# Queries of two heads and two sequences by Strassen's identity, their halves swapped by DMA, with a new plan of the steps

## The chip, the cores and the metric

The kernel runs on one core of a Trainium2 chip. A core has five engines that run their own instruction streams side by side: TensorE (matmul; PE in the profile, its weight loads PEld), VectorE (DVE), ScalarE (ACT), GpSimd (POOL) and SyncE (SP, which here only issues DMAs). The metric is the device time of one execution in microseconds (us), as the median of several runs.

## The reference

All of it is float32. `x` is 16 sequences of 256 tokens by 256. One attention block and one feed-forward block follow each other, each with a layer norm before and after and a residual:

```python
q = (x @ Wq.T).reshape(b, n, H, D)          # H = 16 heads, D = 128
kv_head = cumsum(kv_head * exp(log_f_cumsum), axis=1)
kh, vh = kv_head[..., :H], kv_head[..., H:] # one factor for each token and head
k = einsum('bnd,bnh->bnhd', kp, kh); v = einsum('bnd,bnh->bnhd', vp, vh)
q = rope(q); k = rope(k)
p = softmax(where(mask, einsum('bnhd,bmhd->bhnm', q, k) * scale, -inf))
o = einsum('bhnm,bmhd->bnhd', p, v).reshape(b, n, H * D) @ Wout.T
...
x = x + layernorm(attention(layernorm(x)))
x = x + layernorm(ffn(layernorm(x)))        # ternary weights, silu(gate) * up, rms norm
```

`rope(q)` turns each query: with the halves a and b of its 128 elements, (a cos - b sin, b cos + a sin).

## The kernel before, in words

**Tiling.** The 16 sequences are taken two at a time, in 8 pairs (`Pair`, bp 0 to 7); a pair has 16 heads (`Head`), so there are 128 heads in a row, g = 0 to 127. Operands stand transposed: `xnT` holds a pair's normalised tokens as 128 partitions x 2 chunks of E x 512 columns (256 tokens of each of two sequences). `After` is what follows the attention of one sequence: the output projection (`project_heads`, L833), residual, and the feed-forward block.

**One head.** `queries` (L640) multiplies two 128x128 blocks of `wq_sb` with the two chunks of `xnT` into `qps` in PSUM, 512 columns wide (`contract`, L330; a float32 product is two instructions in the trace). `Rope` (L342) turns it on VectorE: two multiplications with the sine table, each on 64 partitions and from the other half's partitions (L354), one in place with the cosine table (L362), and an addition to `qT` (L365). `keys` (L668) makes `kT` on GpSimd from `kh`, which a DMA of SP brings (`fetch`, L633). `scores` (L672) does four products per head into `sps`; VectorE takes the row minimum with the mask (L695) and ScalarE the exponential (L705). `divide` (L718) divides on ScalarE, `turn` (L738) transposes 32x32 blocks on VectorE (L741) and moves them by DMA through DRAM (`moved`, L748; four `pT`, L754). `scale_values` (L780) makes `vph` on GpSimd, and `outputs` (L788) multiplies into `ops`, which ScalarE copies to `oT` (L813). In pair 0 and the last two heads TensorE does the turning (`on_pe`).

**Order.** The order of every engine's stream is that of the program (`manual_schedule`). `slot(g)` (L1441) is the work of one place in the row of heads: it divides, turns and scales the values of head g - 1, scores head g, makes queries of head g + 1 and keys of head g + 2, rotates the queries of g + 1, and does the outputs of g - 2. All other steps are put in between by `put` (L371): a slot, one of six places in it, and a key, by which the table `MOVED` shifts a step by so many places. DMAs of one engine wait in order: behind a DMA of SP that waits for its data stand all later ones of SP. Per pair and sequence, GpSimd also does the subtraction `lo` (L942), the sums of squares (L960, L1013), normalisations (L308) and residuals (L866, L1063); VectorE does moments (L279), `h` (L931) and `finish` (L1048).

**Buffers.** `heads` has 10 buffers of `oT`, `pT` and `kh` have 3, `xt` (tokens, kept until the last residual) 8, and the four PSUM banks of `ps_mm` are shared by `qps`, `sps`, `gps`, `ups` and others in turn.

**Ternary weights.** During pair 0 `Ternary` (L195) quantises 12 blocks of feed-forward weights: casts and combination on GpSimd (L215, L235 to L238), comparisons on VectorE (L226, L229).

Of the kernel before, what the change touches and what calls it, by code (L numbers as in the profile page):

```python
# [12 lines left out]
MOVED = {  # L13
    "A.fac": 1, "A.y0": 2, "E.fin": 1, "E.mom": -6, "E.nor": 2, "E.pc1": 4, "E.pj0": -1,
    "E.pj1": -1, "E.pj2": 2, "E.pj3": -3, "E.split": 7, "E.sq0": 7, "E.sq1": 3, "E.sq3": 3,
    "E.ss": -3, "E.ssd": -3, "E.sto": 6, "E.tp": 3, "E.up0": -1, "E.up1": -1, "L0": -6,
    "O.fold": 6, "O.g2": -1, "O.g3": -1, "O.gd0": 2, "O.hid1": -2, "O.hid2": -1, "O.lm": 6,
    "O.pj0": -3, "O.pj1": 2, "O.pj3": 3, "O.silu": -3, "O.split": 1, "O.sq0": 1, "O.sq1": 4,
    "O.tp": -1, "O.up0": -3, "O.up1": -3, "O.up2": -7, "O.up3": -3, "P.dec": 2, "P.gate": 2,
    "P.keep0": 1, "P.keep1": 2, "P.kp": -4, "P.ksin": -1, "P.sum": -3, "P.tp0": -2, "P.vhd": 6,  # L20
    "Q.gate": 1, "Q.keep0": 1, "Q.keep1": 4, "Q.kr": -2, "Q.ksin": -2, "Q.mom0": -6,
    "Q.mom1": -3, "Q.nor0": -3, "Q.nor1": 5, "Q.raw": 4, "Q.rows": -3, "Q.sig": -1, "Q.sum": 1,
    "Q.tp0": -1, "Q.tp1": 4, "Q.val": -3, "Q.vh": -6, "Q.vhd": -1, "T0.cb": 1, "T0.ld": -1,
    "T0.ma": -7, "T0.su": 1, "T1.cb": 4, "T1.ld": -4, "T1.ma": -6, "T1.na": -4, "T10.ld": -6,
    "T10.wr": 4, "T11.co": 1, "T11.ma": -2, "T11.na": -3, "T11.su": 1, "T2.ma": -1, "T2.wr": 4,
    "T3.wr": 2, "T4.cb": 1, "T4.ld": 1, "T5.co": 1, "T5.ld": -6, "T5.na": -7, "T7.cb": 1,
    "T7.ld": -3, "T7.ma": -6, "T7.na": -3, "T7.su": -4, "T7.wr": 7, "T8.ld": -10, "T8.su": 1,
    "T8.wr": 7, "T9.ld": -10, "T9.ma": -4, "T9.na": -1, "W0.0": 1, "W0.14": 1, "W1.10": 1,
    "W1.6": -1, "W1.9": 1, "W7.2": -1, "Y12.fin": -4, "Y12.fold": 4, "Y12.nor": 2,
    "Y12.pj0": 3, "Y12.pj1": 2, "Y12.split": 1, "Y12.sq0": 5, "Y12.sq1": 2, "Y12.sq2": -1,  # L30
    "Y12.sq3": 1, "Y12.tp": -7, "Y12.up2": -4, "Y13.nor": 4, "Y13.split": 17,
}

F32 = mybir.dt.float32
BF16 = mybir.dt.bfloat16
F32R = mybir.dt.float32r
AF = mybir.ActivationFunctionType
# [27 lines left out]
def sandwich_kernel(  # L65
# [1375 lines left out]
    def slot(g):  # L1441
# [6 lines left out]
        if before:  # L1448
            before.divide()
# [75 lines left out]
```

## Time and profile before

| | |
|---|---|
| median of 3 runs | 1075.77 us (1074.62 to 1077.19) |
| the profiled execution | 1076.04 us, of which the span from first to last instruction is 1073.8 |
| granted clock of TensorE | 0.997 |
| busy time, us | PE 1058.2, PEld 854.0, DVE 844.8, ACT 734.8, POOL 670.7 |
| DMA | 137.34 MB, mean 128 GB/s |
| 128x512 kT on GpSimd (L670) | 128 of 1.284 us |
| rotation of queries (L354, L362, L365) | 0.688 (64 partitions), 0.700, 0.692 us |

An instruction's row gives its line, engine, operation, the tiles written and read, the shapes, the count, the busy time and the mean in ns of one, and behind a second bar the idle time of its engine ahead of it and what ended that. Matmuls are pipelined: the mean of one is longer than its share of time, so the chain of waits is the better price. "A <- B" in a list of waits says that A's engine idled until B was done; the numbers are the sum in us, the count and the longest.

### The profile page before, as it was taken

How to read it: one execution, taken by the hardware profiler on the slowest of the kernel's cores; microseconds unless marked ns; L12 is line 12 of the kernel's file. 1: busy time of each engine (PE TensorE's matmuls, PEld its weight loads, DVE VectorE, ACT ScalarE, POOL GpSimd, SP SyncE). 2: the span in 40 equal slices, each digit the busy share in tenths (PEclk: the TensorE clock that was granted, in tenths of full speed). 3: DMA queues.
4: the chain of work that ended last, by engine and by line, in shares of the span. 5: the costliest groups of instructions: out<-in, count | busy, mean ns of one | idle time of the engine just before them, and what ended most of it. 6: DMA issues, size and time to landing. Idle time of an engine off the chain costs nothing.

```text
span 1073.8 us, 18504 instructions
## 1 busy us (share of the span) xinstructions
PE 1058.2 (99%) x5730; PEld 854.0 (80%) x5730; DVE 844.8 (79%) x2308; ACT 734.8 (68%) x2152; POOL 670.7 (62%) x705
## 2 busy tenths in 40 slices
PE   8999999999999999999999999999999999999997
PEld 6777776788788877888778887788878888788897
DVE  7888999877887779878798778977788777876565
ACT  4878776676776668576585766866677675857664
POOL 6966897348555676458665585665855546737443
PEclk9999999999999999999999999999999999999998
DMA  7312234553443444444343444435444444443200
GB/s 238 110 51 80 60 121 150 158 162 118 152 143 125 158 130 145 143 130 153 128 157 120 150 140 133 152 130 159 132 137 145 128 142 129 156 133 110 70 11 30
DMA packets 108657, 137.34 MB, mean 128 GB/s; under 512 B 12240, under 2 KB 76240, under 8 KB 108560
## 3 DMA queue, kind: packets, MB, share of 16 engines
q1 hardware_dynamic: 105856, 129.15, 38.0%
q0 software_dynamic: 2000, 6.56, 1.8%
q8 instruction: 46, 0.75, 0.3%
q10 hardware_dynamic: 704, 0.46, 0.1%
q14 instruction: 51, 0.42, 0.1%
HBM read 88.41 MB, written 47.71 MB: 127 GB/s over the span
## 4 chain that ended last, share of the span: by engine, by line
PE 86%; DVE 6%; POOL 4%; ACT 3%; issue 1%; DMA 0%; DVEq 0%; POOLq 0%
PE att L842 18%; PE qps L332 18%; PE sps L682 13%; PE ops L798 9%; PE ffn L997 5%; PE ups L896 5%; PE gps L896 5%; PE ops L805 5%; PE vps L332 1%; PE kp L332 1%; ACT prob L705 1%; DVE prob L695 1%; DVE turned_q L354 1%; PE tps L768 1%; PE tp_f L325 1%
## 5 line engine op out<-in xcount | busy, mean ns | idle before, releaser
L695 DVE CUSTOM_DVE_ANT_0 prob<-sps,mask 128x128 f32<-128x128 f32 (+1 forms) x512 | 160.7, 354 | 117.5 <-PE sps L682 114.7
L813 ACT COPY oT<-ops 128x512 f32<-128x512 f32 x128 | 74.9, 585 | 257.0 <-PE ops L805 256.9
L332 PE MATMUL qps<-xnT,wq_sb 128*128 128x512 f32 x512 | 241.7, 594 | 0.8
L842 PE MATMUL att<-wout_sb,oT 128*128 128x256 f32 x1024 | 237.7, 379 | 0.0
L705 ACT ACTIVATE prob<-prob,low 128x128 f32<-128x128 f32 (+1 forms) x512 | 225.7, 444 | 12.7 <-DVE low L695 12.5
L842 PEld LDWEIGHTS att<-wout_sb,oT 128*128 128x128 f32 x1024 | 188.4, 190 | 30.2 <-issue 8.6
L782 POOL TENSOR_TENSOR vph<-vp,vh 128x512 f32<-128x512 f32 x110 | 115.7, 1052 | 144.6 <-PE ops L805 144.4
L682 PE MATMUL sps<-kT,qT 128*128 128x128 f32 (+1 forms) x1024 | 191.5, 330 | 3.4 <-DVE qT L365 2.5
L354 DVE TENSOR_TENSOR turned_q<-qps,sin_sb 64x512 f32<-64x512 f32 (+1 forms) x258 | 176.0, 682 | 15.7 <-PE qps L332 10.3
L670 POOL TENSOR_TENSOR kT<-kh,kr 128x512 f32<-128x512 f32 x128 | 164.3, 1284 | 8.0 <-PE sps L682 7.7
L734 ACT ACTIVATE even<-prob,total 128x128 f32<-128x128 f32 (+1 forms) x440 | 164.0, 448 | 1.1 <-DVE total L716 1.1
L682 PEld LDWEIGHTS sps<-kT,qT 128*128 128x128 f32 x1024 | 145.1, 191 | 17.0 <-issue 4.0
L332 PEld LDWEIGHTS qps<-xnT,wq_sb 128*128 128x128 f32 x512 | 95.3, 190 | 71.3 <-issue 61.2
L798 PE MATMUL ops<-pT,vph 128*128 128x256 f32 x440 | 131.3, 380 | 0.7 <-POOL lo L942 0.7
L942 POOL TENSOR_TENSOR lo<-h,hi 128x512 fp32r<-128x512 f32 x54 | 68.9, 1276 | 93.4 <-ACT hi L940 84.4
L741 DVE STREAM_TRANSPOSE sq<-even 128x768 f32<-128x768 f32 x110 | 107.4, 976 | 11.1 <-ACT even L734 7.3
L705 ACT ACTIVATION_READ_ACCUMULATOR prob<-prob,low 128x1 f32 x512 | 97.2, 190 | 0.0
L362 DVE TENSOR_TENSOR qps<-qps,cos_sb 128x512 f32<-128x512 f32 (+1 forms) x129 | 89.5, 694 | 4.6
L805 PEld LDWEIGHTS ops<-pT,vph 128*128 128x128 f32 x440 | 83.5, 190 | 11.4
L365 DVE TENSOR_TENSOR qT<-qps,turned_q 128x512 f32<-128x512 f32 (+1 forms) x129 | 88.4, 686 | 4.5
L805 PE MATMUL ops<-pT,vph 128*128 128x128 f32 x440 | 84.5, 274 | 0.0
L798 PEld LDWEIGHTS ops<-pT,vph 128*128 128x128 f32 x440 | 73.8, 191 | 9.3 <-issue 3.4
(177 smaller groups left out, 1894.7 us busy)
## 6 DMA issues: line engine op xcount, KB each, us to landing
moved<-sq SPq DMA_DIRECT2D x110, 384.0 KB, 2.3
pT<-moved SPq DMA_DIRECT2D x440, 96.0 KB, 2.2
kh<-rows SPq DMA_DIRECT2D x126, 256.0 KB, 3.3
xt<-in_x_dram SPq DMA_DIRECT2D x14, 256.0 KB, 2.9
out_dram<-y POOLq DMA_DIRECT2D x13, 256.0 KB, 3.3
wout_sb<-in_wout_dram SPq DMA_DIRECT2D x2, 1024.0 KB, 9.6
w_gu<-in_wgu_dram POOLq DMA_DIRECT2D x8, 256.0 KB, 3.5
wq_sb<-in_wq_dram SPq DMA_DIRECT2D x1, 1536.0 KB, 10.3
```

The lines of the kernel that those rows point to most:

```text
L332: nc.tensor.matmul(ps, lhs[:, c, :], rhs[:, c, :], start=(c == 0), stop=(c == EC - 1))
L354: self.engine.tensor_mul(by_sequence(self.turned[a : a + HALF, :]), by_sequence(self.src[b : b + HALF, :]), over_sequences(sin_sb[b : b + ...
L670: nc.gpsimd.tensor_mul(self.kT, self.kh, self.pair.kr)
L682: nc.tensor.matmul(sps[:, cols], self.qT[:, n0 + i * P : n0 + (i + 1) * P], self.kT[:, n0 : n0 + (i + 1) * P], start=True, stop=True,)
L695: nc.vector.tensor_tensor_reduce(out=prob[:, cols], in0=sps[:, cols], in1=mask[:, P - i * P :], scale=-SCALE, scalar=F32_MAX, op0=ALU.add, ...
L705: nc.scalar.activation(prob[:, cols], prob[:, cols], AF.Exp, bias=low[:, i : i + 1], scale=-1.0, accum_out=self.total[:, b * 2 + i : b * 2 ...
L734: nc.scalar.activation(dst, src, AF.Copy, scale=self.total[:, 2 * b + i : 2 * b + i + 1])
L741: nc.vector.transpose(turned.rearrange("p k u q -> p (k u q)"), self.even.rearrange("p k u q -> p (k u q)"),)
L782: nc.gpsimd.tensor_mul(self.vp, self.pair.vp, self.pair.vh[:, :, self.h : self.h + 1].to_broadcast([P, NT, D]),)
L798: nc.tensor.matmul(ops[:, n0 : n0 + N], self.vp[:, b * (N // P), :], early, start=True, stop=False,)
L805: nc.tensor.matmul(ops[:, n0 + P : n0 + N], self.vp[:, b * (N // P) + 1, :], late, start=False, stop=True,)
L842: nc.tensor.matmul(self.acc[:, t, :], oT[:, n0 + t * P : n0 + (t + 1) * P], wout_sb[:, h, :], start=(h == 0 and t == 0), stop=(h == H - 1) ...
```

## The change

For pairs 1 to 7, heads are taken by twos (`Two`). With the two heads' weights as a 2x2 matrix of blocks (w11 and w12 the two chunks of the first head, w21 and w22 of the second) and the tokens as x11, x12 (first chunk, two sequences), x21, x22 (second chunk), the 2x2 product of blocks takes seven products of 256 columns instead of eight. Four differences of tokens for each pair are made on GpSimd (`token_sums`), and three sums of weights once, on VectorE during pair 0 (`weight_sum`; the sum w21 + w22 overwrites w21 in `wq_sb`).

```diff
+        def first_products(self):
+            self.ps = mm_tile([P, BP, N], f"q1_{self.name}")
+            self.product(self.ps[:, 0, :], w11, x11, True)
+            self.product(self.ps[:, 1, :], w12, x21)
+        def first_out(self):
+            self.part = p1.tile([P, N], F32, tag="part", name=f"part1_{self.name}")
+            nc.scalar.copy(self.part, self.ps[:, 0, :])
+        def first_sum(self):
+            nc.vector.tensor_add(
+                self.heads[0].qT[:, :N], self.ps[:, 1, :], self.part
+            )
+        def second_product(self):
+            self.product(self.ps[:, 0, :], s2, self.pair.sums_of_tokens[1])
+        def second_out(self):
+            self.part = p1.tile([P, N], F32, tag="part", name=f"part_{self.name}")
+            nc.scalar.copy(self.part, self.ps[:, 0, :])
+        def third_products(self):
+            self.ps = mm_tile([P, BP, N], f"q2_{self.name}")
+            self.product(self.ps[:, 0, :], s1, t1, True)
+            self.product(self.ps[:, 1, :], s3, t3)
+        def third_out(self):
+            self.parts = p1.tile([P, BP, N], F32, tag="parts", name=f"parts_{self.name}")
+            nc.scalar.copy(self.parts, self.ps)
+        def third_sums(self):
+            dst = self.heads[1].qT[:, N:]
+            nc.gpsimd.tensor_add(dst, self.parts[:, 0, :], self.parts[:, 1, :])
+            nc.gpsimd.tensor_add(dst, dst, self.part)
+        def last_products(self):
+            self.product(self.ps[:, 0, :], s4, x22)
+            self.product(self.ps[:, 1, :], w22, self.pair.sums_of_tokens[3])
+        def last_sums(self):
+            nc.vector.tensor_add(
+                by_sequence(middle[:, N : 3 * N]),
+                self.ps,
+                over_sequences(self.part, BP),
+            )
+        def swap(self):
+            for half in range(2):
+                a, b = half * HALF, (1 - half) * HALF
+                nc.sync.dma_start(
+                    out=turned_ring[a : a + HALF, :, :],
+                    in_=queries_ring[b : b + HALF, i : i + 2, :],
+                )
```

The queries stand in a ring of four in SBUF (`queries_ring`), and the swapped halves of two heads in `turned_ring`. The second products of a bank add onto the first, which a copy on ScalarE has taken out. The rotation works on SBUF alone:

```diff
+        def rotate(self):
+            q, turned = by_sequence(self.qT), by_sequence(self.turned)
+            nc.vector.tensor_mul(turned, turned, over_sequences(sin_sb, BP))
+            nc.vector.tensor_mul(q, q, over_sequences(cos_sb, BP))
+            nc.vector.tensor_sub(self.qT, self.qT, self.turned)
```

The plan has twelve places in a slot instead of six, and the steps of the heads are put into it as the others are, with keys of their own in `MOVED` (cut here, as is the table, whose old entries are mostly doubled or moved):

```diff
+        two = twos.get(g + 2 + g % 2)
...
+        if two:
+            steps = (
+                (two.third_products, two.third_out),
+                (two.first_products, two.first_out),
+            )[g % 2]
+            for step, name in zip(steps, ("Z", "Zs")):
+                put(g, "begun", step, key=movable(name))
...
+        for b in range(BP):
+            put(g, "scores", lambda b=b: head.scores(b))
+        if two and g % 2:
+            put(g, "begun", two.first_sum, key=movable("Zt"))
+            put(g, "probed", two.second_product, key=movable("Zp"))
+            put(g, "probed", two.second_out, key=movable("Zo"))
+        elif two:
+            put(g, "probed", two.last_products, key=movable("Zp"))
...
+        if two and g % 2 == 0:
+            put(g, "probed", two.last_sums, key=movable("Zo"))
+            put(g, "probed", two.third_sums, key=movable("Zt"))
...
+        if after and g + 1 >= H:
+            put(g, "rotated", after.rotate, key=movable("O"))
...
+        if two and g % 2 == 0:
+            put(g, "rotated", two.swap, key=movable("Zw"))
```

So a two's first and second products stand in the odd slot three before its first head, its third and last products, sums and swaps in the even slot two before, ahead of and behind that slot's scores. Its rotations stand one slot before each head.

Smaller parts:

```diff
-    heads = ctx.enter_context(tc.tile_pool(name="heads", bufs=10))
+    heads = ctx.enter_context(tc.tile_pool(name="heads", bufs=7))
...
-        xts[q] = p3.tile([P, N // P, E], F32, tag="xt", name=f"xt_{q}", bufs=8)
+        xts[q] = p3.tile([P, N // P, E], F32, tag="xt", name=f"xt_{q}", bufs=5)
...
+    def load_again(q):
+        xts[q] = p3.tile([P, N // P, E], F32, tag="xt", name=f"xt2_{q}", bufs=5)
+        nc.sync.dma_start(out=xts[q], in_=x[q].rearrange("(t p) e -> p t e", p=P))
...
-            nc.gpsimd.tensor_copy(self.wb, self.w)
+            nc.scalar.copy(self.wb, self.w)
...
-            nc.gpsimd.tensor_sub(up, up, self.dn)
+            nc.vector.tensor_sub(up, up, self.dn)
...
-            turned = p2.tile([P, 4, 3 * BP, 32], F32, tag="sq32", name=f"sq32_{self.tag}")
+            turned = p1.tile([P, 4, 3 * BP, 32], F32, tag="sq32", name=f"sq32_{self.tag}")
...
-            self.pT = p3.tile([P, 4, 3 * BP, 32], F32, tag="pT", name=f"pT_{self.tag}")
+            self.pT = p2.tile([P, 4, 3 * BP, 32], F32, tag="pT", name=f"pT_{self.tag}")
...
-                nc.vector.tensor_scalar(
+                nc.scalar.activation(
                     self.y[:, t, :],
                     self.acc[:, t, :],
-                    rs[:, t : t + 1],
-                    nb[:, t : t + 1],
-                    ALU.mult,
-                    ALU.add,
+                    AF.Identity,
+                    bias=nb[:, t : t + 1],
+                    scale=rs[:, t : t + 1],
                 )
```

Tokens are loaded a second time for the residual (`load_again`, in the slot 17 after a pair's start), which frees their first buffer. The last step is `finish`, which goes from VectorE to ScalarE. The tiles `xhi` and `xlo` have one buffer each instead of two, apart from two of the last sequences, which take the buffers of `xnT`. The ones are a single column that is broadcast, and ten warm-up products of 128 columns replace five of 256.

## The prediction

> **What bounds the kernel now.** I read the share of each engine first, then the busy time by stretch, then the chain of work in one pair's steady part, then the costs by shape.
>
> ```profile
> PE 1058.2 (99%) x5730; PEld 854.0 (80%) x5730; DVE 844.8 (79%) x2308; ACT 734.8 (68%) x2152; POOL 670.7 (62%) x705
> ...
> PE 86%; DVE 6%; POOL 4%; ACT 3%; issue 1%; DMA 0%; DVEq 0%; POOLq 0%
> ```
>
> TensorE is busy 99% and carries 86% of the chain. The busy time by stretch (after each stretch's length: PE, PEld, DVE, ACT, POOL) shows where it is not full:
>
> ```profile
> 120.00:188.00 68.00, 65.47 (x312) 48.76 (x312) 62.50 (x163) 47.33 (x151) 58.40 (x57) 1.00 0.37 117
> ...
> 445.00:573.20 128.20, 128.04 (x696) 103.74 (x695) 102.45 (x282) 87.86 (x257) 80.61 (x85) 1.00 0.44 140
> ```
>
> A pair of 16 slots lasts 128.2 us (8.01 us a slot) and TensorE idles 0.16 us of it. From 120 to 188 us, with VectorE busy 62.5 of 68 us (92%) and GpSimd 58.4 (86%), TensorE idles 2.5 us (3.7%). The waits of that stretch name the cause, and the chain from 502 us on has the prices of matmuls:
>
> ```profile
> PEld sps L682 <- DVE qT L365: 2.7, 3, 2.0
> ```
> ```profile
> 507.70 3.45 PE att L842 x16
> ...
> 512.46 1.31 PE sps L682 x8
> ```
>
> Every f32 product is two instructions. Sixteen of 256 columns take 3.45 us, 0.2156 each; four query instructions of 512 take 1.72 in the chain of waits, 0.430 each. So time goes by columns, and a 256-column instruction is half a 512-column one; its weight load (190 ns) fits beneath it.
>
> **The products.** Two heads take 8 instructions of 512 columns now, 8 x 0.430 = 3.44 us, and 14 of 256 afterwards, 14 x 0.2156 = 3.02. That is 0.42 us for two heads; 56 such twos in pairs 1 to 7 give **-23.6 us**, and a pair would last 128.2 - 8 x 0.42 = 124.8. Six more weight loads for two heads (190 ns) would cost 1.1 us if bare; the att row, with a new weight for each instruction, excludes that. Pair 0 keeps its products.
>
> **VectorE.** The groups by shape in 445 to 573.2 us:
>
> ```profile
> L354 DVE TENSOR_TENSOR turned_q<-qps,sin_sb 64x512 f32<-64x512 f32 x32 | 22.0, 688 | 1.2 <-PE qps L332 0.5
> ...
> L362 DVE TENSOR_TENSOR qps<-qps,cos_sb 128x512 f32<-128x512 f32 x16 | 11.2, 700 | 0.6
> L365 DVE TENSOR_TENSOR qT<-qps,turned_q 128x512 f32<-128x512 f32 x16 | 11.1, 692 | 0.6
> ```
>
> These 44.3 us go, and the 1.9 us of finish (L1053) move to ScalarE. Added per pair: 48 rotations of 128x512 at 0.69 (33.1 us), 8 sums of 256 columns at 0.42 (3.4) and 8 of 512 at 0.69 (5.5). Together 102.4 - 46.2 + 42.0 = 98.2 of 124.8 us. On the face of it VectorE gets lighter.
>
> But the kind of operand changes: the old steps read qps in PSUM and one table in SBUF, the rotations read two tensors in SBUF. The trace has a few such instructions beside a busy GpSimd, the compare steps of the ternary weights (minimum, median, maximum ns):
>
> ```profile
> L226 DVE SCALAR_TENSOR_TENSOR t_gu<-t_gu x8: 691/706/1746, 34.1 to 109.2; 128x512 bf16<-128x512 bf16 x8
> ```
> ```profile
> L229 DVE SCALAR_TENSOR_TENSOR t_p<-t_p x4: 684/1372/2059, 124.0 to 152.9; 128x512 bf16<-128x512 bf16 x4
> ```
>
> The one of 1746 ns began at 102.09 us, 0.1 us after a kT on GpSimd (101.99, 1.29 us), and ended at 103.84, 0.56 after kT's end; those with GpSimd idle take 0.69. They stand in line for each other, and GpSimd stretches too: the kT at 153.93 took 1.72 instead of 1.28. Over the 24 of L226 and L229 the mean is (7.8 + 8.4 + 2.8 + 5.5)/24 = 1.02 us, 0.33 above 0.69. The bounds for a rotation are therefore 0 and 1.3 us of waiting (a whole kT); I take 0.33, since GpSimd was about as busy then (88.0 of the first 120 us, 58.4 of the next 68) as it will be. That is 48 x 0.33 = 15.8 us, so VectorE holds 114 of 124.8 us (91%): its spare time falls from 1.6 to 0.7 us a slot.
>
> The Trainium skill (SBUF — State Buffer, Who interferes with whom) says that a VectorE instruction with two SBUF inputs and a GpSimd instruction that reads SBUF block each other for the whole instruction. By it alone GpSimd's 95.2 us and 33.1 of rotations would follow one another, 128.3 us a pair, and nothing would be gained. The trace agrees for the big operations; the subtraction at 1039.92 us took 0.68 beside a GpSimd pow of 0.71, so small ones do not hold it.
>
> **GpSimd.** Per pair 16 adds and 4 token differences of 128x256 at 0.73 (row of L1013, 724 to 732 ns): 80.6 + 14.6 = 95.2 us (76%). Nothing on the path if kT, vph and the third sums stay within their slot of slack; an even slot carries 1.28 + 1.46 + 1.05 and 2.8 of feed-forward work, 6.6 of 7.8 us.
>
> **ScalarE.** Per two, two copies of 256 columns (0.46, the PSUM row of L773) and one of 512 (0.585, L813): 12 us a pair, with finish (4 x 0.57) 102 of 124.8 us; it idles 35.7 us a pair for ops now, which hides them. One is on a path: the last products add into the bank that third_out reads. Third products take 0.86 us, the scores 1.31, so the copy must end by 2.17 us in the slot. It begins near 1.06 and ends near 1.65; with one feed-forward cast (0.61) ahead, 2.26. I take 0.05 us for each two, 2.8 in all (bounds 0 and 0.5 each, 28).
>
> **SP and the swaps.** SP's list shows, for the slot whose scores start at 504.5 us, the fetch at 505.03, moved at 507.58 and the four pT from 509.96 to 511.70, 7.2 us in. Divide and turn come 1.5 us later after the change (0.86 of products, 0.59 of copy), so SP reaches the swaps at 8.7; issues of 0.38 each, and a landing of 3.3 (the kh row, 256 KB each as well), end at 12.7. The rotation's place in the next slot is 7.8 + 4.5 = 12.3: 0.4 us late, of which nothing waits on TensorE yet: three rotations (2.07 + 1.0) end at 15.8, and the scores that need them start at 15.6 + 0.86 = 16.5. Behind the swaps on SP stand the next fetch and moved (due at 12.1), which are not held up. I take 0; the ends are 0 (it can only add) and 34 (rival 3). The reloads of x (16 of 256 KB, 2.9 us) and fewer buffers of oT, pT, xt and sq32 cost nothing: the loads are asked for three slots ahead, pT is written one slot after its predecessor's reader; uncovered, one reload would cost its 2.9 us.
>
> **Pair 0, start and end.** Eight sums of weights (0.69, 5.5 us) and 12 ternary differences come to VectorE, which idles 20.6 of the first 120 us; hidden, and 5.5 us if not. Casts leave GpSimd (12 x 0.6) for ScalarE, idle 32 us there. The end's steps keep their order; single buffers of xhi and xlo may hold a split for some tenths: 0, at most 1 us.
>
> **What becomes late.** The scores wait for qT where VectorE is crowded. The one wait of 1.8 us (164.2 us, the hand-over between pairs, with statistics of four tiles ahead of the rotation) is what VectorE at 92% cost. I put one such wait into each of the seven pairs, less the 0.86 us of products that now stand ahead of the scores: 7 x 0.95 = 6.7 us. Ends: the steady stretch's 0.16 us a pair (1.1 in all), and 3.7% of 7 x 124.8 (32 us).
>
> **Sum**, against the profiled execution's own 1076.04 us (span 1073.8 and 2.2 around it; 0.27 over the median 1075.77): 1076.0 - 23.6 + 6.7 + 2.8 = 1061.9, less the 0.3 to the median: **1061.6 us**.
>
> **Rivals.**
> 1. *All of it is hidden*: rotations wait for GpSimd only in spare time. 1075.8 - 23.6 + 1.1 = 1053. For it: 0.7 us a slot stays spare, and scores now have products ahead. Against: the waits at 92%.
> 2. *The shared access of VectorE and GpSimd becomes the bound*, slower than before. If a rotation waits half a kT (0.64 us), VectorE needs 98.2 + 30.7 = 128.9 us a pair, 0.7 over now: 1081; by the idle share of 120 to 188 us, 1075.8 - 23.6 + 32 = 1084. I put it at 1083. It decides from 0.62 us of mean wait, where 98.2 + 48 w reaches 128.2. For it: maxima of 2.06 us. Against: half the rows at 0.69.
> 3. *The swaps come late*: if they land in 4.6 us (rows of the first loads) and 0.7 of slack is used up, each two costs 0.6 us, 34 in all: 1086.
> 4. *It gives back what it takes*: waits of some 24 us, 1076.
>
> Chances: forecast 0.40 (own range 1054 to 1071), rival 1 0.24, rival 2 0.24, rival 3 0.06, rival 4 0.06. Faster by over 0.2% (2.2 us, about what a measurement here tells from no change): 0.64; within 0.06; slower 0.30. The range takes rival 1's floor less one us of luck at the ends, 1051, and from rivals 2 and 3 all but the worst, to 1090.
>
> **What would show it.** Right: qps groups of 256 columns, about 784 instructions at 0.216 in the chain, a steady pair of 125 to 127 us, rotations with means near 1.0 us and maxima of 1.7 to 2.1, and TensorE idle before sps with qT as releaser. Wrong: rotations at 0.69 throughout (rival 1), means above 1.3 with VectorE over 95% (rival 2), VectorE waiting for the swap's DMA (rival 3), or last products waiting for the copies. A different clock would void the sum.

## The result and the profile after

The changed kernel takes 1154.38 us (median of 4 runs, 1149.02 to 1156.4) against 1075.19 for the kernel before beside it (4 runs): a ratio of 1.0726, 95% interval 1.0683 to 1.0769. It is slower by 79 us, where 14 us less (1061.6) were forecast. The profiled execution took 1156.24 us, of which the span is 1154.5.

The page of the changed kernel, engine shares and chain of waits:

```profile
PE 1067.5 (92%) x6076; PEld 920.5 (80%) x6076; DVE 913.1 (79%) x2302; ACT 821.5 (71%) x2358; POOL 835.8 (72%) x821
...
PE 39%; DVE 25%; POOL 14%; DMA 9%; ACT 7%; issue 4%; SPq 2%; DVEq 0%; POOLq 0%; ACTq 0%
```

TensorE's part of the chain fell from 86 to 39%. No other engine is full: VectorE is busy 79%, as before. So this is no engine that became the bound, but a chain through several engines that TensorE now waits for. The busy time of one steady pair (pair 4; columns as in the stretches above):

```profile
582.80:718.00 135.20, 127.24 (x744) 111.77 (x744) 108.64 (x278) 99.62 (x285) 107.53 (x104) 1.00 0.56 168
```

It lasts 135.2 us, not 128.2, and TensorE is without work for 8.0 us of it. The rotations and kT, by shape over the whole span:

```profile
L820 POOL TENSOR_TENSOR kT<-kh,kr 128x512 f32<-128x512 f32 x128 | 182.8, 1430 | 0.3
...
L815 DVE TENSOR_TENSOR queries_ring<-queries_ring,cos_sb 128x512 f32<-128x512 f32 x112 | 128.2, 1144 | 0.0
...
L816 DVE TENSOR_TENSOR queries_ring<-queries_ring,turned_ring 128x512 f32<-128x512 f32 x112 | 123.2, 1100 | 3.9
...
L814 DVE TENSOR_TENSOR turned_ring<-turned_ring,sin_sb 128x512 f32<-128x512 f32 x112 | 97.7, 873 | 40.9 <-DMA turned_ring<-queries_ring 40.9
```

A rotation step takes (873 + 1144 + 1100)/3 = 1039 ns, near the 1.02 of the prediction, and kT 1430 instead of 1284. The last row has what the prediction put at nothing: VectorE idles 40.9 us for the swap's DMA. The list of waits says for whom that matters (sum in us, count, longest):

```profile
PE sps L832 <- DVE total L868: 25.4, 23, 2.9
...
PE sps L832 <- DVE queries_ring L816: 14.6, 12, 3.2
PE q L675 <- DVE queries_ring L702: 12.0, 15, 3.1
```

The scores (sps) wait for the last step of a rotation (L816). The first line is the same wait: in all 23 cases L868, a reciprocal of 0.17 us, stands directly behind L816 on VectorE, and the wait is put down to what came last. The timeline of one slot of pair 4 shows the whole chain, for SyncE, VectorE, GpSimd and TensorE (start, duration, line, tiles; idle time ahead in brackets):

```profile
666.23 1.74 SPq L906 DMA_DIRECT2D pT<-moved  x4
668.09 1.11 SPq L748 DMA_DIRECT2D turned_ring<-queries_ring  x2
```
```profile
672.60 0.74 DVE L814 TENSOR_TENSOR turned_ring<-turned_ring,sin_sb 128x512 f32<-128x512 f32 x1 [1.96 <-DMA turned_ring<-queries_ring]
673.26 1.75 DVE L815 TENSOR_TENSOR queries_ring<-queries_ring,cos_sb 128x512 f32<-128x512 f32 x1
675.05 1.42 DVE L816 TENSOR_TENSOR queries_ring<-queries_ring,turned_ring 128x512 f32<-128x512 f32 x1
```
```profile
672.75 1.72 POOL L820 TENSOR_TENSOR kT<-kh,kr 128x512 f32<-128x512 f32 x1
674.43 1.49 POOL L934 TENSOR_TENSOR vph<-vp,vh 128x512 f32<-128x512 f32 x1
```
```profile
676.61 1.55 PE L832 MATMUL sps<-kT,queries_ring 128*128 128x128 f32 x8 [2.24 <-DVE total L868]
```

SyncE issues the swaps behind the four pT at 668.09; they land near 672.5; VectorE, idle since 670.6, starts then, at the same moment as kT and vph on GpSimd; two of its steps take 1.75 and 1.42 us instead of 0.69; and TensorE stands for 2.24 us.

Two sums over the matmuls of a trace keep the account. A matmul's own time runs from its start, or the end of the one before it if that is later, to its end; the rest is idle. A pair runs from its first copy of oT to the next pair's, pair 7 to its own last copy. Both sums run over these eight pairs; the 28 us ahead of them and the 54 to 55 us behind, alike in both kernels, are left out.

| us | pair 0 | pair 1 | mean of pairs 2 to 6 | pair 7 | TensorE own | idle |
|---|---|---|---|---|---|---|
| before | 123.9 | 119.1 | 128.0 | 108.3 | 984.7 | 6.8 |
| after | 144.1 | 135.9 | 135.9 | 111.9 | 992.5 | 78.6 |

So of some 80 us, 37.0 are in pairs 0 and 1, 39 in pairs 2 to 6 and 3.6 in pair 7; 71.8 are idle time of TensorE, and its own time grew by 7.8 although each pair from 1 on has 4096 columns fewer to multiply (counted over both instructions of a product; the last section takes this apart).

### The profile page after: what moved, and what is told of

Its sections match the earlier page's. It is cut to its first block, busy times and chain, and to the rows that moved or that the text cites. A ratio compares the mean times of both kernels' runs of the same rounds, so it can differ in the third digit from the quotient of the medians.

```text
span 1154.5 us, 19837 instructions
## 1 busy us (share of the span) xinstructions
PE 1067.5 (92%) x6076; PEld 920.5 (80%) x6076; DVE 913.1 (79%) x2302; ACT 821.5 (71%) x2358; POOL 835.8 (72%) x821
## 4 chain that ended last, share of the span: by engine, by line
PE 39%; DVE 25%; POOL 14%; DMA 9%; ACT 7%; issue 4%; SPq 2%; DVEq 0%; POOLq 0%; ACTq 0%
PE att L994 9%; DMA turned_ring<-queries_ring 7%; PE q L675 6%; PE sps L832 6%; PE ops L950 4%; DVE queries_ring L815 4%; DVE queries_ring L816 4%; DVE turned_ring L814 3%; PE gps L1052 3%; PE ffn L1161 3%; DVE sq L893 2%; PE ops L957 2%; PE ups L1052 2%; POOL kT L820 2%; ACT even L886 2%
## 5 line engine op out<-in xcount | busy, mean ns | idle before, releaser
L832 PE MATMUL sps<-kT,queries_ring 128*128 128x128 f32 (+1 forms) x1024 | 199.9, 337 | 55.7 <-DVE total L868 25.4
L832 PEld LDWEIGHTS sps<-kT,queries_ring 128*128 128x128 f32 x1024 | 149.4, 193 | 90.6 <-DVE queries_ring L816 17.7
L847 DVE CUSTOM_DVE_ANT_0 prob<-sps,mask 128x128 f32<-128x128 f32 (+1 forms) x512 | 155.2, 351 | 44.9 <-PE sps L832 43.3
L820 POOL TENSOR_TENSOR kT<-kh,kr 128x512 f32<-128x512 f32 x128 | 182.8, 1430 | 0.3
L934 POOL TENSOR_TENSOR vph<-vp,vh 128x512 f32<-128x512 f32 x110 | 127.9, 1163 | 65.5 <-PE ops L957 63.4
L814 DVE TENSOR_TENSOR turned_ring<-turned_ring,sin_sb 128x512 f32<-128x512 f32 x112 | 97.7, 873 | 40.9 <-DMA turned_ring<-queries_ring 40.9
L815 DVE TENSOR_TENSOR queries_ring<-queries_ring,cos_sb 128x512 f32<-128x512 f32 x112 | 128.2, 1144 | 0.0
L816 DVE TENSOR_TENSOR queries_ring<-queries_ring,turned_ring 128x512 f32<-128x512 f32 x112 | 123.2, 1100 | 3.9
L1103 POOL TENSOR_TENSOR lo<-h,hi 128x512 fp32r<-128x512 f32 x54 | 77.5, 1434 | 50.1 <-ACT hi L1101 43.0
L675 PE MATMUL q<-xs,sums_of_weights 128*128 128x256 f32 x224 | 68.4, 387 | 12.0 <-DVE queries_ring L702 12.0
L727 POOL TENSOR_TENSOR queries_ring<-parts 128x256 f32<-128x256 f32 x56 | 46.9, 837 | 36.0 <-ACT parts L723 36.0
```

Source lines behind the costliest of these rows:

```text
L675: nc.tensor.matmul(out, weights, tokens, start=first, stop=True, skip_group_check=True)
L814: nc.vector.tensor_mul(turned, turned, over_sequences(sin_sb, BP))
L815: nc.vector.tensor_mul(q, q, over_sequences(cos_sb, BP))
L816: nc.vector.tensor_sub(self.qT, self.qT, self.turned)
L820: nc.gpsimd.tensor_mul(self.kT, self.kh, self.pair.kr)
L832: nc.tensor.matmul(sps[:, cols], self.qT[:, n0 + i * P : n0 + (i + 1) * P], self.kT[:, n0 : n0 + (i + 1) * P], start=True, stop=True,)
```

## The experiments

Theory **P**: the rotations read two tensors in SBUF and stand in line with GpSimd, and this lengthens the path to the scores. Theory **S**: the swaps land late. Theory **W**: the steps moved to VectorE at the start (ternary casts and differences) cost the first 200 us. The kernel before took 1076.2 to 1076.9 us beside the runs. Pair times and idle time are those of each run's one profiled execution, the medians those of all its executions.

| run | median, us | ratio to before, 95% interval | pair 0 | pair 1 | mean of pairs 2 to 6 | idle |
|---|---|---|---|---|---|---|
| e1_one_input | 1110.73 | 1.0290 to 1.0391 | 141.9 | 127.7 | 130.3 | 47.1 |
| e2_no_swap | 1134.82 | 1.0523 to 1.0554 | 141.5 | 133.9 | 132.3 | 63.8 |
| e3_neither | 1086.10 | 1.0075 to 1.0105 | 139.0 | 127.2 | 127.1 | 31.8 |
| e4_ternary_back | 1160.93 | 1.0721 to 1.0829 | 142.1 | 137.7 | 136.9 | 82.6 |
| e5_swap_on_gpsimd | 1201.57 | 1.1119 to 1.1203 | 146.1 | 146.1 | 141.5 | 108.4 |
| e6_no_weight_sums | 1155.71 | 1.0708 to 1.0794 | 137.8 | 137.5 | 136.3 | 77.9 |
| e7_early_one_input | 1081.48 | 1.0033 to 1.0070 | 132.1 | 125.4 | 127.6 | 27.7 |
| e8_old_places | 1159.73 | 1.0724 to 1.0802 | 140.8 | 136.9 | 135.2 | 73.5 |
| e9_swap_first | 1170.70 | 1.0846 to 1.0889 | 142.4 | 138.9 | 137.6 | 85.1 |
| e10_second_late | 1158.94 | 1.0702 to 1.0803 | 142.4 | 132.7 | 135.1 | 75.0 |
| e12_tables_in_psum | 1191.96 | 1.1020 to 1.1158 | 150.6 | 135.8 | 140.1 | 105.1 |
| e13_three_banks | 1261.18 | 1.1666 to 1.1741 | 154.7 | 141.3 | 150.2 | 140.5 |
| e14_ring_of_four | 1132.44 | 1.0484 to 1.0538 | 139.2 | 135.9 | 131.8 | 60.4 |
| e15_early_second_late | 1083.68 | 1.0043 to 1.0083 | 133.1 | 123.2 | 127.8 | 28.0 |
| e16_ring_one_input | 1094.55 | 1.0142 to 1.0185 | 137.7 | 126.6 | 128.4 | 36.7 |
| e17_ring_kept_sums | 1133.10 | 1.0501 to 1.0558 | 142.4 | 136.1 | 131.9 | 61.5 |
| e18_early_old_places | 1081.09 | 1.0025 to 1.0049 | 129.6 | 125.3 | 127.1 | 25.9 |

**The operands of the rotations (e1).**

```diff
-            nc.vector.tensor_mul(turned, turned, over_sequences(sin_sb, BP))
-            nc.vector.tensor_mul(q, q, over_sequences(cos_sb, BP))
-            nc.vector.tensor_sub(self.qT, self.qT, self.turned)
+            nc.vector.transpose(self.turned, self.turned)
+            nc.vector.transpose(self.qT, self.qT)
+            nc.vector.transpose(self.qT, self.turned)
```

> The three rotations of a head become three transposes of 32x32 blocks over the same 512 columns, in the same places with the same waits, each with one input in SBUF. The rotary embedding is left out (the queries that are scored are not turned), all else is computed. Theory P (two SBUF inputs stand in line with GpSimd): a rotation falls from a mean of 1.02 to about 0.7 us with no maximum over 0.8, GpSimd's kT from 1.43 to 1.28 us, a steady pair from 136 to about 129 us, the whole from 1154 to about 1105. Theory S (the swapped halves come late): the waits for the swap stay and the whole stays above 1140. Theory W (VectorE's extra work in pair 0): the first 200 us keep their 37 us either way.

1110.73 us, 44 less. The steps took 0.67 to 0.71 us and kT 1.28 again:

```profile
L819 POOL TENSOR_TENSOR kT<-kh,kr 128x512 f32<-128x512 f32 x128 | 163.7, 1280 | 1.1 <-DMA kh<-rows 0.8
...
L815 DVE STREAM_TRANSPOSE queries_ring<-turned_ring 128x512 f32<-128x512 f32 x112 | 79.7, 712 | 3.8
L813 DVE STREAM_TRANSPOSE turned_ring<-turned_ring 128x512 f32<-128x512 f32 x112 | 78.2, 698 | 76.5 <-DMA turned_ring<-queries_ring 76.4
L814 DVE STREAM_TRANSPOSE queries_ring<-queries_ring 128x512 f32<-128x512 f32 x112 | 74.9, 669 | 0.0
```

VectorE's wait for the swaps rose to 76.4 us without costing that much, so it is partly the time won. Theory S, which expected over 1140, is not enough by itself. A transpose is another operation than a product; e12 below keeps the operation and changes only where one operand lies.

**The swaps (e2) and both together (e3).** In e2 the two DMAs are gone and the sine step reads q itself, still two SBUF inputs:

```diff
-            nc.vector.tensor_mul(turned, turned, over_sequences(sin_sb, BP))
+            nc.vector.tensor_mul(turned, q, over_sequences(sin_sb, BP))
...
-        if two and g % 2 == 0:
-            put(g, "rotated", two.swap, key=movable("Zw"))
```

> The swaps' 112 DMAs are left out, and the product with the sine table reads the query itself instead of its swapped halves, so the rotary embedding is wrong in that term; the instruction, its two SBUF inputs and its place stay. Theory S: VectorE's 41 us of waiting for the swap go, SP is free earlier, a steady pair falls from 136 to about 130 us and the whole to about 1115. Theory P: rotations still take 1.02 us, the waits move to them, and the whole stays above 1135.

> Both edits together: transposes with one SBUF input in place of the rotations, and no swap DMAs (the rotary embedding is left out). If P and S are together the loss of the steady pairs, a pair comes down to 125 to 127 us, the 124.8 that TensorE's products allow and a little, and the whole to 1075 to 1090, where what is left over 1052 is the loss of the first 200 us. If pairs stay above 130, a third cause is in them (the copies of ScalarE ahead of the products, or GpSimd's sums).

20 us for the swaps (1134.82, between what S and P expected of e2), 68 for both, close to 44 + 20. Neither theory alone is enough: P has two thirds, S one third. The steady pairs of e3 take 127.1 us, somewhat over the 125 to 127 expected: in pair 4 TensorE's own time is 125.2 us and it idles 2.0, so of the 3.4 us forecast for a pair 0.9 is left. Pairs 0 and 1 keep 23 us.

**The ternary steps (e4).**

```diff
-            nc.scalar.copy(self.wb, self.w)
+            nc.gpsimd.tensor_copy(self.wb, self.w)
...
-            nc.vector.tensor_sub(up, up, self.dn)
+            nc.gpsimd.tensor_sub(up, up, self.dn)
```

> The two steps of the ternary weights that moved go back to GpSimd (the cast from ScalarE, the difference up - dn from VectorE); nothing is left out. Theory W: GpSimd no longer stands idle behind the difference (59 us of such waits in the run after), the first 200 us lose about 20 of their 37 us, and the whole falls to about 1132. If the loss there is by the sums of weights or by the first twos, the whole stays within 8 us of 1154. Pairs 2 to 6 stay at 136 us.

Nothing is won by moving them back, so W, tested in this way, gets no support.

**The swaps from another queue (e5).** `nc.gpsimd.dma_start` instead of `nc.sync.dma_start` in `swap`.

> The two swaps of each two heads are issued from GpSimd's queue instead of SyncE's; nothing else differs. Theory S (the swaps are late because SyncE issues them only after it has waited for moved and issued the four pT transfers) expects at least half of the 20 us that leaving the swaps out gave back: 1144 or less, VectorE's wait for turned_ring from GpSimd's issue below the 41 us of the changed kernel. Rival: the path is as long on GpSimd, since its own adds, kT and vph stand ahead of the issue and a transfer from there takes longer to land: 1150 to 1165, with GpSimd waiting for VectorE's sums.

47 us slower, well beyond the rival's 1150 to 1165. The swaps' issue now stands in GpSimd's own stream, ahead of later kT and vph; GpSimd idles 113.4 us ahead of it (27.0 put down to L868, the step behind a rotation's last; for 85.5 the profile names no cause). VectorE's wait for turned_ring rose to 63.4 us, and the transfers took 4.4 us to land (3.7 from SyncE). The direction is the rival's, that the path is as long on GpSimd; what of it makes the 47 us was not separated.

**The swaps ahead of pT (e9), and a deeper ring (e14, e17).** In e9 only SyncE's order differs; `turned_in` is the part of `turn` that issues the four pT:

```diff
+            if not (two and g % 2 == 0):
+                put(g, "probed", before.turned_in, key=movable("R"))
...
-            put(g, "rotated", two.swap, key=movable("Zw"))
+            put(g, "rotated", two.swap)
+            if before and not before.on_pe:
+                put(g, "rotated", before.turned_in)
```

> Only SyncE's order in the even slots differs: moved, then the two swaps, then the wait for moved and the four pT, instead of moved, its wait, pT, swaps. In the changed kernel's slot at 661 us the sums were done at 662.25 and SyncE waited for moved from 662.61 to 666.20, so the swaps can be issued at about 662.7 and land 5.4 us earlier. Theory S expects VectorE's 41 us of waiting for turned_ring to fall under 5 and the time to fall by the 15 to 20 us that leaving the swaps out gave back: 1134 to 1140. Rival: pT, which goes 1.1 us later behind the swaps and shares the DMA engines with them, becomes late for ops: 1148 or more with TensorE waiting for pT.

16 us slower, although VectorE's wait for turned_ring fell from 40.9 to 21.7 us. The waits of e9 say why:

```profile
PE ops L952 <- DMA pT<-moved: 50.1, 25, 5.0
```
```profile
SPq L748 <- DVE queries_ring L816: 188.3, 55, 13.2
```

SyncE now stands at the swap for 188 us, waiting for L816: turned_ring holds two heads, so a swap for the next two may not overwrite it before the second rotation of the last two has read it, and that rotation belongs to the same slot. Behind SyncE's wait stands pT. In the slot shown above the sums were ready at 662.25, but the rotation that read the old contents ended at 665.66, 0.6 us before pT's turn: the order on SyncE hid the true limit. e14 and e17 keep e9's order and give the ring four heads; to make room e14 leaves out the sums of weights, and e17 has five buffers of oT instead of seven:

```diff
-    turned_ring = const.tile([P, BP, T], F32, name="turned_ring")
+    turned_ring = const.tile([P, 4, T], F32, name="turned_ring")
...
-                    out=turned_ring[a : a + HALF, :, :],
+                    out=turned_ring[a : a + HALF, i : i + 2, :],
```

> turned_ring holds four heads instead of two, the swaps are issued ahead of the wait for moved and of pT, and the sums of weights are left out of the computation to make room in SBUF (the control with that alone: 1155.7 us). Theory S2 (a swap can't start before the rotation of the same slot has read the old contents of the two-deep ring) expects VectorE's wait for turned_ring under 5 us, pT no later than before, and 15 to 20 us under the control: 1135 to 1141. Rival: the transfers themselves, 256 KB each, hold pT back whatever the order: 1150 or more, TensorE waiting for pT.

> The ring of four with the swaps ahead of pT and everything computed; oT has five buffers instead of seven to make room. Theory S2: 15 to 20 us under the changed kernel, 1134 to 1140, still 5% slower than the kernel before, since the operands of the rotations cost 44 us. Rival: five buffers of oT are too few and stop the copies of outputs: 1150 or more, ScalarE or TensorE waiting for a projection.

1132.44 us (23 under its control e6), and 1133.10 with everything computed, 21 under the changed kernel, a little beyond what was expected. The row of e17 that answers to the 40.9 us:

```profile
DVE turned_ring L814 <- DMA turned_ring<-queries_ring: 4.2, 4, 1.6
```
```profile
PE ops L952 <- DMA pT<-moved: 16.9, 12, 4.8
```

S2 holds for the time and for VectorE's wait. Its "pT no later than before" doesn't: TensorE waits 16.9 us for pT in e17 (16.0 in e14), where the changed kernel's list has no such wait, so the 21 us are a net gain and a part of the rival is true. e17 is the fastest form found that computes everything, and still 5.0 to 5.6% slower than the kernel before. A ring of four with SyncE's old order was not run.

**Tables in PSUM (e12, with its control e13).** e13 has three banks in `ps_mm` instead of four, e12 also uses the fourth for copies of the tables:

```diff
+    tables_ps = ps_t.tile([P, 2, N], F32, tag="t", name="tables_ps")
...
-            nc.vector.tensor_mul(turned, turned, over_sequences(sin_sb, BP))
-            nc.vector.tensor_mul(q, q, over_sequences(cos_sb, BP))
+            nc.vector.tensor_mul(turned, turned, over_sequences(tables_ps[:, 0, :], BP))
+            nc.vector.tensor_mul(q, q, over_sequences(tables_ps[:, 1, :], BP))
```

> The sine and cosine tables that the rotations read are copied to PSUM once, so two of the three rotation steps read one operand from PSUM and one from SBUF; one of the four PSUM banks for products pays for it. Theory P (two SBUF operands are what makes VectorE and GpSimd stand in line) expects these two steps at 0.69 to 0.75 us (0.87 and 1.14 before), the third still near 1.1, and a time 20 to 30 us under that of the kernel with three banks and the tables in SBUF. Rival: any VectorE step beside GpSimd stretches, or the time is set elsewhere: the two steps stay above 0.85, or the time is within 6 us of that kernel.

> The changed kernel with three instead of four PSUM banks for products: the control for the kernel with the tables in PSUM. If the fourth bank is hardly used, 1150 to 1162; if scores, sums and products wait for a bank, 20 us or more over the changed kernel's 1154.

The same arithmetic with one operand elsewhere, in e12:

```profile
L826 DVE TENSOR_TENSOR queries_ring<-queries_ring,turned_ring 128x512 f32<-128x512 f32 x112 | 110.5, 987 | 3.9
...
L825 DVE TENSOR_TENSOR queries_ring<-queries_ring,tables_ps 128x512 f32<-128x512 f32 x112 | 75.8, 677 | 0.0
L824 DVE TENSOR_TENSOR turned_ring<-turned_ring,tables_ps 128x512 f32<-128x512 f32 x112 | 74.9, 669 | 21.2 <-DMA turned_ring<-queries_ring 21.1
```

and with both in SBUF, in e13:

```profile
L815 DVE TENSOR_TENSOR queries_ring<-queries_ring,cos_sb 128x512 f32<-128x512 f32 x112 | 128.2, 1145 | 0.0
...
L814 DVE TENSOR_TENSOR turned_ring<-turned_ring,sin_sb 128x512 f32<-128x512 f32 x112 | 93.5, 835 | 15.0 <-DMA turned_ring<-queries_ring 14.9
```

The two steps that read PSUM take 0.67 and 0.68 us (0.84 and 1.15 in e13); the one that still reads two SBUF tensors takes 0.99. The kernel is 69 us faster than e13, well beyond the 20 to 30 expected: probably because with fewer banks TensorE can do less ahead, so that each late rotation costs more; this is not shown. The bank itself costs 107 us, so this is no way out.

**The swap without the operands (e16).** e14 with e1's edit.

> As the ring of four without sums of weights, and the three steps of a rotation are VectorE instructions with one SBUF input (the rotary embedding is left out of the computation); the swaps stay. If the operands and the late swap are together the whole loss of the steady pairs, pairs 2 to 6 take 126.5 to 128.5 us each as they do without swaps, and the time is 1078 to 1090. If the transfers of the swaps cost something besides, pairs 2 to 6 stay at 130 or more and the time at 1100 or more.

Pairs 2 to 6 take 128.4 us, at the upper end of what the two causes together leave, and 1.3 over e3. The time is 4.6 us over the first range, far from the second, and 8.5 over e3. The transfers seem to cost a little besides, for TensorE waits 17.1 us for pT here and 5.8 in e3; but e16 also has the other order on SyncE and no sums of weights, so this is not shown.

**Pairs 0 and 1 (e6, e7, e8, e10, e15, e18).** The trace of the changed kernel shows VectorE behind TensorE there. At 116.9 us a compare step of the ternary weights is caught between GpSimd's instructions, and the first sum of two heads, for which the second product waits, stands behind it:

```profile
116.90 3.42 DVE L251 SCALAR_TENSOR_TENSOR t_gu<-t_gu 128x512 bf16<-128x512 bf16 x1
120.24 0.41 DVE L702 TENSOR_TENSOR queries_ring<-q,part 128x256 f32<-128x256 f32 x1
```
```profile
120.80 0.67 PE L675 MATMUL q<-xs,sums_of_weights 128*128 128x256 f32 x2 [3.10 <-DVE queries_ring L702]
```

Four single causes were tried, e4 above among them. e6 leaves the eight `weight_sum` steps out (the products read `w11`, `w12`, `w22` in their place); e8 gives the keys of the ternary weights and of pair 1 their old slots and places:

> The eight sums of weights are left out of the computation; the products read the weights themselves in their place. Theory W2 (pairs 0 and 1 are long because the eight steps, about 9 us of VectorE, stand in front of the steps that TensorE waits for) expects pair 0 and pair 1 together 10 to 20 us shorter than the 280.0 us of the changed kernel, 1135 to 1144 in all. Theory B (the compare steps of the ternary weights and the rotations, stretched by GpSimd, are the cause) and theory C (the new order of the early steps is) expect at most 5 us from it, 1149 or more.

> The steps of the ternary weights and of pair 1's preparation go back to the slots and places that they had in the kernel before; the rest of the new plan stays. Theory C (the new order of the early steps lengthens pairs 0 and 1) expects pair 0 and pair 1 together at least 10 us shorter than the 280.0 us of the changed kernel, 1144 or less. Theories P, B and W2 expect them within 6 us of 280.0 or longer, 1148 or more, since the same instructions meet GpSimd elsewhere.

e6 shortened pair 0 by 6.3 us, pair 1 became 1.6 longer, and the time is the changed kernel's, so W2 is not met; e8 took 2.3 us off both pairs and nothing off the time. e10 moves the second product:

```diff
-            put(g, "probed", two.second_product, key=movable("Zp"))
-            put(g, "probed", two.second_out, key=movable("Zo"))
+            put(g, "projection", two.second_product)
+            put(g, "projection", two.second_out)
```

> The second product of each two heads and its copy stand behind the projection matmuls of their slot instead of ahead of them; nothing else differs. Theory Q (in pairs 0 and 1 VectorE is some us behind TensorE, and the second product, which waits for VectorE's first sum, now stops TensorE ahead of 3.4 us of projection that needs nothing from that slot) expects pairs 0 and 1 together 8 to 15 us shorter than 280.0, no long gap ahead of the second product (12 us of such waits in the changed kernel), and 1138 to 1147 in all. Rival: TensorE then waits as long at the next step that needs VectorE, or the bank held longer delays scores: pairs 0 and 1 within 4 us of 280.0, 1149 or more.

Pairs 0 and 1 are 4.9 us shorter, between the theory and its rival, and the median shows no gain. e7 takes e3 and makes the early steps of VectorE one-input (the four sums of weights, the two compare steps and the difference), e15 adds e10's edit to that, e18 adds e8's:

```diff
-            nc.vector.tensor_sub(s3, w11, w21)
+            nc.vector.tensor_scalar(s3, w11, 1.0, 0.5, ALU.mult, ALU.add)
...
-            nc.vector.tensor_sub(up, up, self.dn)
+            nc.vector.transpose(up, self.dn)
```

> As the kernel without swaps and with one-input rotations (1086.1 us; pair 0 139.0, pair 1 127.2 us), and besides the sums of weights, the two compare steps and the difference of the ternary weights are VectorE instructions with one SBUF input in the same places: the rotary embedding, the sums of weights and the ternary values are left out of the computation. Theory P for the start as well (two SBUF inputs on VectorE stand in line with GpSimd) expects pair 0 at 124 to 130 and pair 1 at 119 to 123, 1066 to 1073 in all. Theory C (the order of the early steps) expects pair 0 at 136 or more and 1080 to 1088.

> The kernel without swaps, with one-input rotations and one-input early steps (1081.5 us; TensorE idle 7.3 and 9.0 us in pairs 0 and 1), and besides the second product and its copy behind the projection of their slot. Rotary embedding, sums of weights and ternary values are left out of the computation. Theory Q expects the idle time of pairs 0 and 1 to fall from 16.3 us to under 10 and 1072 to 1077 in all. Theory C (the order of the early steps delays VectorE, wherever TensorE then waits) expects 13 or more and 1079 to 1084.

> The kernel without swaps, with one-input rotations and one-input early steps (1081.5 us; TensorE idle 16.3 us in pairs 0 and 1 together), and besides the steps of the ternary weights and of pair 1's preparation at the slots and places that they had in the kernel before. Rotary embedding, sums of weights and ternary values are left out of the computation. Theory C (what is left of the early loss is the new order of these steps) expects the idle time of pairs 0 and 1 at 10 us or less and 1073 to 1077. If the rest comes from the products that now stand between the old steps, or from several small waits, it stays at 13 or more and the time at 1079 to 1085.

e7 is 4.6 us faster than e3 and pairs 0 and 1 are 8.7 us shorter. That fits the same contention, but it is less than P expected (pair 0 at 130 at most, 1073 in all), and the time lies in C's range; e18 then speaks against C. Neither the second product's place nor the order of the early steps moved the rest: idle time in the two pairs is 16.3 us in e7, 15.1 in e15, 15.1 in e18, and the times lie within 3 us.

## Why the prediction was wrong, point by point

**The products: right.** In pair 3, query products take 24.8 us of TensorE's own time in e3 (112 of 0.221 us) against 28.0 before: 3.2 less, where 3.4 was forecast (25.0 in pair 4 of the changed kernel). TensorE's whole own time in that pair fell from 128.0 to 125.2.

**The stretch of the rotations: right in size.** 1.04 us against 1.02; VectorE is busy 108.6 us of pair 4, where 114 was worked out, and 94.9 in e3, without the stretch, where 98.2 was. The 1.02 is a mean of 24 steps of another kind, so that it came so close is partly luck.

**The step that failed is "What becomes late".** It turned that stretch into one wait of 1.8 us for a pair, less 0.86 of cover, 6.7 us in all. The one-input rotations show 44 (e1), 0.39 for each of the 112 heads. The mistake was to ask how full VectorE is. At 80% it has room for all of it, but a rotation starts when the swap has landed and GpSimd is in its way, and the scores wait for its end: up to 1.05 us more (three steps, 0.35 each on average) falls on the path in a slot where the rotation is the last thing before the scores. The one old wait of 1.8 us measured a different plan, in which a query was rotated from PSUM and ready early. For the same reason rival 2, whose mechanism this is, had the wrong threshold: it was to decide from VectorE's full load, 128.2 us of work, and the loss came at 108.6.

**"The swaps: I take 0" failed too.** 20 us (e2), 21 when it is mended (e17). The working had the landing 12.7 us behind the slot's scores and the scores that need it at 16.5, 3.8 later, for a rotation of 3.1, which left 0.7 of slack. In the slot shown (its scores began at 658.49) the landing came at about 14.0 and those scores were due at 15.9: 1.9 us for a rotation that took 3.9. It missed that the swaps write a ring that the rotation of the same slot still reads: with two heads in the ring no order on SyncE could issue them before 665.7 in this slot, 2.4 us ahead of their place, and e9 shows that going there costs more than it gives. Measured: the two issues take 1.11 us and the landing 3.7, for 0.76 and 3.3 assumed. Rival 3 had this loss at 34 and a chance of 0.06.

**"Pair 0 ... hidden, 5.5 us if not" failed.** Pairs 0 and 1 lost 37.0 us. Rotations and swaps are 13.8 of them (e3), the other two-input steps of VectorE 8.7 (e7). Of the remaining 14.5, TensorE's own time in pair 0 has 3.4 (125.0 against 121.6; query products have 30.5 against 27.5, since those for pair 1 are begun there), and idle time 11.8 in both pairs, less 0.7 in pair 1's own time. What sets that idle time stays open. The place of the second product (e15) and the order of the early steps (e18) are excluded as single causes; that it is many small waits is only argued.

**Smaller terms.** The last products' wait for third_out, 2.8 in the sum, shows as 0.4 us of idle time ahead of them. GpSimd is busy 107.5 us of a steady pair, not 95.2 (95.0 in e3, with the same instructions), since its own instructions stretch too. The reload of x and the fewer buffers, put at nothing, were not tested singly; e3, which has them, idles 2.0 us in pair 4, so they and all else together cost a steady pair no more than that. The clock was supposed to stay full and did not (below).

## What to carry to other kernels

Price a slower step by the path from its input's arrival to its first reader, not by the share of its engine: with VectorE 80% busy TensorE idled 8 us of a steady pair. When operands move from PSUM to SBUF, count each instruction that then reads two SBUF tensors beside GpSimd, here 0.35 us more on average than 0.69, and GpSimd's own longer too (kT 1.43 instead of 1.28). For a DMA into a reused buffer look for the last reader of the old contents before looking at the queue; with too few buffers an earlier place in the queue makes it worse (e9), with enough it pays (e17).

## What the runs showed of the hardware that was not expected

**Half clock after short gaps.** The changed kernel has, ahead of its last 12 us, seven windows of 3.41 us in which TensorE's granted clock is 0.5; the kernel before has none there. Two stretches, the second right behind the gap of 3.10 us shown above (length, PE, PEld, DVE, ACT, POOL, granted clock, DMA share, GB/s):

```profile
117.60:121.00 3.40, 0.30 (x2) 0.23 (x2) 3.40 (x5) 0.69 (x3) 2.16 (x3) 1.00 0.39 118
121.00:124.40 3.40, 3.40 (x9) 1.63 (x9) 0.76 (x6) 2.64 (x11) 0.00 (x0) 0.65 0.12 36
```

The four query instructions at 121.63 us took 3.26 us instead of the 1.88 of those at 110.27. Six of the windows follow a single gap of 2.06 to 3.18 us, one follows gaps of 1.27 and 1.11 close together; gaps of 2.17 us at 155.8, 2.92 at 399.9 and 2.24 at 674.4 had none behind them. What differs is where a gap lies: all seven windows begin on one grid of 3.413 us, and the stretch of the grid ahead of each holds 2.06 to 2.88 us of idle time of TensorE. From 30 us to the last copy of oT no other stretch holds more than 1.99; the gap of 2.92 us is cut by the grid into 1.99 and 0.93. In the other runs the two groups overlap between 1.60 and 2.00 us (stretches behind a half-clock window left aside), and above 2.00 half clock always followed.

Seven windows cost at most 7 x 3.41/2 = 12 us. They are not all of why TensorE's own time grew by 7.8 us: a matmul behind a gap overlaps with none before it. In pair 4, at full clock, the 128 score instructions take 23.1 us of own time, 21.2 in e3; eight of them stand behind gaps, 0.36 us each, where the mean in e3 is 0.17. With each kind of matmul at its median own time, an estimate from these traces, the matmuls take 21.9 us less than before, half clock adds 12, and those behind gaps 17 more than before. The windows are also a likely reason for the spread of the runs (1149.02 at a mean clock of 0.992, the others at 0.984 to 0.986 up to 1156.4), so differences of 5 us between medians of kernels with such gaps show little. The Trainium skill (TensorE: Matmul & The Clock Gate, Part 1: The HAM clock gate) puts the half clock behind an idle window of about 3.4 us that runs free of the kernel; the windows' length and grid agree, while here some 2.1 us of idle time in one, three fifths, were enough.

**One operand in PSUM is enough.** 0.67 us against 0.84 and 1.15 for the same instruction (e12, e13). The Trainium skill (SBUF — State Buffer, Who interferes with whom) says that VectorE with at most one SBUF input, outside certain fast modes, doesn't contend with GpSimd; these rows and e1's agree. Its rule of whole instructions in line, by which nothing would be gained, was the better warning than the mean of the few early rows. The prediction's reading that small GpSimd operations don't hold VectorE is borne out, but they are held themselves: 22 of the 336 rotation steps met only GpSimd instructions on two columns and took 0.66 to 0.69 us, while GpSimd's pow took up to 1.18 beside them instead of 0.72.

**The fourth bank.** Three PSUM banks for products instead of four cost 107 us (e13): ahead of the scores TensorE waits 47.0 us for VectorE's L847, which reads the scores out of their bank; with four banks the list has no such wait.
